# Layer 1 of a spatial CNN: adding the residual in place, permuting into the residual's own tile, and one ring of five tiles

## The chip, the cores and the metric

The kernel runs on one core of one Trainium2 chip. The metric is the device time of one execution in microseconds (us). Before the change it is 4453.58 us, the median of three runs (4452.78 to 4460.18). Profiles are of one further execution each; in them times count from the first instruction.

The core has five engines with an instruction stream each: TensorE (PE, with its weight loads PEld), VectorE (DVE), ScalarE (ACT), GpSimd (POOL) and SyncE (SP). SyncE here only issues DMAs; ScalarE issues some too, in between its own work. An issued DMA is carried out by 16 DMA engines. An instruction waits on semaphores at the head of its engine's stream, and what stands behind it in that stream waits as well.

## The reference, cut to what matters

The input is x with shape (32, 48, 64, 128): batch, channels, height H, width W, in float32. Two layers follow each other, with different weights. Each is a residual block:

```python
x = x + scnn(group_norm(x, 16 groups))       # layer 0
x = x + scnn(group_norm(x, 16 groups))       # layer 1

def step(w, b):
    def f(carry, inp):
        nxt = inp + conv1d(carry, w, b)      # 5 taps, 48 -> 48 channels, padding 2
        return nxt, nxt
    return f
# scnn: down over H, up over H (same weights), right over W, left over W
```

Each of the four passes is a scan: row h needs the finished row h-1 (or h+1), and column v needs v-1 (or v+1). The convolution of a row step runs along the width, that of a column step along the height. So the work is a chain of 126 row steps and 254 column steps for each group of batches, and a step is a small matrix product followed by an addition.

## The kernel before, in words

Batches are taken in groups of eight (GB), four groups. Row phases treat one group, column phases treat two groups (a pair) at once. The list PHASES gives twelve phases: eight of rows and four of columns; the last two are ("cols", 1, 0) and ("cols", 1, 1), the column scans of layer 1 for the first and for the second pair. With these alone the change is concerned. A scan step is nine matmuls (L647), which add into three PSUM tiles, and three VectorE instructions (L656), which add bias and the old value and write the new column over it in SBUF.

SBUF holds one large tile, the arena: three slots, and behind them a stage of four tiles of 128 x 2048 float32 (1 MB each). A column phase needs its whole width at once in the scan to the right and again in the scan to the left, but there are four quarters of the width (j = 0 to 3) and only three slots. So quarter 0 is written out to DRAM (spill_unit) after its part of the right scan, quarter 3 takes its slot, and in the left scan, when quarter 3 is finished and its results are out, quarter 0 is read back into that slot. The next column phase loads its quarters 0, 1 and 2 (load_unit) into the slots of the finished phase as these come free.

The left scan finishes quarter 3 first, then 2, 1, 0. A quarter consists of six units (UNITS: three channel groups times the two batch groups of the pair) of 128 x 2048 values. For each unit of layer 1 the finished values, in the order of the scan, have to be added to the residual (the layer's input, kept in DRAM as "mid") and brought into the order of the output, in which the eight columns of a block lie side by side. Before, one function does both, add_permuted (L606 to 610): eight GpSimd additions of 128 x 256 each read the scan's values and the residual with permuted strides, and write into a tile perm. The residual lies in one of three tiles nat: two of the stage and a spare one in the memory of the row weights (downs), which layer 1 no longer needs then. The two other stage tiles are perm.

What then happens to perm depends on the phase. In the last phase, and for quarter 3 of the phase before it, store_result (L618) writes it straight to the output in DRAM, in runs of 32 float32 (128 bytes). For quarters 2, 1 and 0 of the first of the two phases, hold_result (L626) writes it as one block of 1 MB to a DRAM buffer (held), issued by ScalarE, and let_result (L630) copies it from there to the output during the next phase. store_result and let_result are issued by SyncE, and so are load_unit and spill_unit. load_residual (L578) is issued by ScalarE in layer 1, three or four DMAs a unit.

The last quarter of the last phase (j = 0, when TensorE has ended) has a treatment of its own. last_loads (L880) loads its six residuals into the slot of the finished quarter 2. last_results (L884) adds them on VectorE in place, then copies each unit in eight slices into a stage tile, by ScalarE, GpSimd and VectorE in turn (L894), and stores it.

The order of each engine's instructions is written out by hand, by an agenda. `at(t, fn, ...)` puts a piece of work at time t, counted in scan steps, not in microseconds; before each step the main loop traces all pieces that are due, and in_order (L196) makes each engine keep this order. The times thus fix the order within each engine's stream only; when a piece really runs is decided by semaphores. In plan_cols (L796) `left` is the step at which the left scan begins. The units of layer 1 stand at left + 34 + 32 per quarter + 4.5 per unit; the first residuals at left + 16; the following ones 4.9 after the unit that frees their tile; a store or hold 5 after its unit; the spill reads of quarter 0 at left + 64 and 2 steps apart; last_loads at left + 97, just ahead of the units of quarter 1.

Every DMA of the built program also waits for an earlier one: eight completion semaphores are used in turn, so a DMA waits for the eighth before it in program order, whichever queue that one is on.

Of the kernel before, what the change touches and what calls it, by code (L numbers as in the profile page):

```python
# [31 lines left out]
ALU = mybir.AluOpType  # L32
# [59 lines left out]
def kernel(  # L92
# [8 lines left out]
    nc = tc.nc  # L101
    B, _, H, W = x.shape
    NK = W // E8
    NH = H // E8
# [5 lines left out]
    UNIT = NH * LINE  # L110
# [22 lines left out]
    def const(shape, name):  # L133
        return cpool.tile(shape, F32, tag=name, name=name)
# [3 lines left out]
    stage = arena[:, 3 * SLOT :].rearrange("p (i n) -> p i n", i=4)  # L138
    wt = {k: const([FULL, NG, NG * FULL], f"w{k}") for k in ("right", "left")}
    downs = const([FULL, 2, NG, NG * FULL], "downs")  # L140
    wt |= {f"down{i}": downs[:, i] for i in range(2)}
    bd = const([FULL, NG, 2, 3], "bd")
    mask_sb = const([P, P], "mask_sb")
    maskp = const([P, NG, FULL], "maskp")
# [74 lines left out]
    def slots(k):  # L219

        return (0, 1, 2) if k % 2 == 0 else (2, 1, 0)
# [327 lines left out]
    UNITS = [(g, half) for g in range(NG) for half in range(2)]  # L549

    def quarter(k, j):
        return slot[slots(k)[j % 3]].rearrange("p (o s n) -> p s o n", s=2, o=NG)
# [29 lines left out]
        for e, c0, c1, p0 in pieces(o):  # L582
            dma(nat[p0 : p0 + c1 - c0], by_col(t, e, j)[c0:c1], nc.scalar if layer else None)

    def add_residual(k, j, i, nat):
        o, half = UNITS[i]
        unit = quarter(k, j)[:, half, o]
        nc.gpsimd.tensor_tensor(unit, unit, nat, ALU.add)  # L588

    def keep_result(k, j, i):  # L590
        _, layer, pair = PHASES[k]
# [7 lines left out]
    def by_image(t):  # L599

        return t.rearrange("p (a e k b) -> p a b k e", a=NH, e=E8, b=GB)

    def by_w(t):
        return t.rearrange("p (a b k e) -> p a b k e", a=NH, b=GB, e=E8)

    def add_permuted(k, j, i, nat, perm):  # L606
        o, half = UNITS[i]
        res = by_image(quarter(k, j)[:, half, o])
        for a in range(NH):
            nc.gpsimd.tensor_tensor(by_w(perm)[:, a], res[:, a], by_image(nat)[:, a], ALU.add)  # L610

    def in_output(j, g, e):

# [4 lines left out]
    def store_result(k, j, i, perm):  # L618
        pair = PHASES[k][2]
        o, half = UNITS[i]  # L620
        for e, c0, c1, p0 in pieces(o):
            dst = in_output(j, 2 * pair + half, e)[c0 * NH : c1 * NH]
            src = perm[p0 : p0 + c1 - c0].rearrange("p (a b n) -> p a b n", a=NH, b=GB)
            dma(dst.rearrange("(c a) b n -> c a b n", a=NH), src)
# [166 lines left out]
    def follows(k):  # L791

        _, layer, pair = PHASES[k]
        return PHASES[k - 1] == ("rows", layer, 2 * pair + 1)

    def plan_cols(k, t0, prev):  # L796
        _, layer, pair = PHASES[k]
        n = 2 * NG
        after = prev == "cols"
        for i in range(n):  # L800
            if follows(k) and UNITS[i][1] == 1:
                other = nc.scalar
# [12 lines left out]
            at(t0 + 50 + 2 * i, load_unit, k, 3, i)  # L815
        final = k == len(PHASES) - 1
        left = t0 + W - 1
        end = left + W - 1
        for i in range(n):
            at(left + 64 + 2 * i, spill_unit, k, i, True)  # L820
        units = []
        for n_done, j in enumerate((3, 2, 1, 0)):
            every = 4.5
            if j == 0 and PHASES[k + 1 if not final else k][0] == "rows":
                every = 7
            units += [(left + 34 + 32 * n_done + every * i, j, i) for i in range(n)]
        stats = None
        if layer == 0:
            stats = ResultStatsV(f"r{2 * pair}"), ResultStatsA(f"r{2 * pair + 1}")
        tiles = [stage[:, i] for i in range(4)]  # L830
        nats, perms = (tiles, None) if layer == 0 else (tiles[0:2], tiles[2:4])
        if layer:
            nats.append(downs.rearrange("p i g n -> p (i g n)")[:, 0:UNIT])
        ahead = len(nats)

        for u, (t, j, i) in enumerate(units):
            nat = nats[u % ahead]
            o, half = UNITS[i]
            if u < ahead:
                at(left + 16, load_residual, k, j, i, nat)  # L840
            elif not (final and j == 0):
                at(units[u - ahead][0] + (3 if layer == 0 else 4.9), load_residual, k, j, i, nat)
            if layer == 0:
                at(t, add_residual, k, j, i, nat)
                at(t + 4, keep_result, k, j, i)
                unit = quarter(k, j)[:, half, o]
                if half == 0:
                    for b in range(GB):
                        at(t + 5 + b, stats[0].take, j, o, unit, b)
                else:  # L850
                    at(t + 1, stats[1].take, j, o, unit)
            elif not (final and j == 0):
                perm = perms[u % 2]
                at(t, add_permuted, k, j, i, nat, perm)
                if final or j not in HELD:
                    at(t + 5, store_result, k, j, i, perm)
                else:
                    at(t + 5, hold_result, j, i, perm)
        if layer == 0:
            t = units[-1][0] + 14  # L860
            g = 2 * pair
            spread(t, scaling(f"r{g}", 1, g, stats[0], r_masks), 1)
            spread(t + 20, scaling(f"r{g + 1}", 1, g + 1, stats[1], r_masks), 1)
        if layer:

            at(left + 10, nc.scalar.copy, junk[:, 0:1], quarter(k, 3)[:, 0, 0, RUN - 1 : RUN])
        if layer and not final:
            todo = [(j, half, e) for j in HELD for half in range(2) for e in range(E8)]
            for n, what in enumerate(todo):
                at(end + 63 + 1.9 * n, let_result, *what)  # L870
        if final:
            at(left + 97, last_loads, k)
            at(end + 4, last_results, k)

    def last_tiles(k):

        s = slot[slots(k)[2]].rearrange("p (i n) -> p i n", i=2 * NG)
        return [s[:, i] for i in range(2 * NG)]
# [5 lines left out]
    def last_results(k):  # L884

        for i, nat in enumerate(last_tiles(k)):
            o, half = UNITS[i]
            unit = quarter(k, 0)[:, half, o]
            nc.vector.tensor_tensor(unit, unit, nat, ALU.add)
            perm = stage[:, i % 4]  # L890
            for a in range(NH):
                eng = (nc.scalar, nc.gpsimd, nc.vector)[a % 3]
                copy = eng.copy if eng is nc.scalar else eng.tensor_copy
                copy(by_w(perm)[:, a], by_image(unit)[:, a])  # L894
            store_result(k, 0, i, perm)


# [3 lines left out]
    for k, (kind, layer, _) in enumerate(PHASES):  # L901
        (plan_rows if kind == "rows" else plan_cols)(k, starts[k], PHASES[k - 1][0])

    def wide_nat(i0, n):
        return arena[0:P, i0 : i0 + GB * n * W].rearrange("p (b m) -> p b m", b=GB)

    tiles = [stage[0:P, i] for i in range(4)]
    nats1 = [wide_nat(2 * SLOT + i * UNIT * 4, 8) for i in range(2)]
    plan_input(1, [starts[0] + 38 + 13 * j for j in range(4)], 11, 5, nats1, tiles[2:4])
    nats = [wide_nat(3 * SLOT, 4)]  # L910
# [214 lines left out]
```

## Time and profile before

| what | before |
|---|---|
| median of three runs | 4453.58 us |
| the profiled execution | 4463.67 us, span 4461.9 us |
| TensorE busy | 4157.1 us, 93% of the span |
| GpSimd additions of add_permuted (L610) | 336 of about 1.09 us |
| ScalarE copies of last_results (L894) | 18 of 0.65 us |
| last matmul ends | 4337.8 us |
| DMA moved | 680 MB, mean 152 GB/s |

How to read what follows. The page gives for every engine the busy time, its share and the number of instructions. It cuts the span into 40 equal slices of 111.5 us and prints the busy share of each in tenths. A group line gives source line, engine, operation, output and inputs with shapes and the number of instructions; after the bar the busy time and the mean of one in ns; after the next bar the idle time of the engine just before them and what ended most of it. A timeline line gives start, length, and in brackets the idle time before with what released it. The waits list says who waited for whom, with total, number and longest. In the table of windows each row is a stretch of the span: its length, busy time and (count) of the engines, granted TensorE clock, busy share of the 16 DMA engines and GB/s. The names tell the phase: step_10r and step_10l are the right and left scans of layer 1's first pair, step_11r and step_11l those of the second.

### The profile page before, as it was taken

The page shows a single profiled execution, that of the slowest core. Times are in us where ns is not written, and L with a number is a line of the kernel's source. Part 1 is how long each engine was busy: PE and PEld are TensorE (multiplying, and loading weights), DVE is VectorE, ACT ScalarE, POOL GpSimd, SP SyncE. Part 2 cuts the span into 40 slices and gives each one's busy share as a digit, 9 for nine tenths or more (in the row PEclk, how much of TensorE's full clock was granted, in tenths as well). Part 3 has the DMA queues.
Part 4 walks back from the last instruction along what each step waited for, and adds up shares of the span by engine and source line. Part 5 has one row for each costly group of instructions (what it writes and reads, how often), then busy time and mean ns, then how long its engine had stood idle before and what let it go on. Part 6 is the DMA issues. An engine that isn't in the chain of part 4 may idle for free.

```text
span 4461.9 us, 89843 instructions
## 1 busy us (share of the span) xinstructions
PE 4157.1 (93%) x36632; PEld 4127.5 (93%) x36632; DVE 2187.4 (49%) x6594; ACT 1190.5 (27%) x2360; POOL 908.3 (20%) x943
## 2 busy tenths in 40 slices
PE   4899997999999999998999999999999999999980
PEld 1799997999999999998999999999999999999980
DVE  5354443446655444444446654444444444444442
ACT  1743301434785545100006765403000000000000
POOL 3342000324322020000004410000000035520544
PEclk9999998999999999999999999999999999999995
DMA  8989789856988989578308989658295059999799
GB/s 175 177 166 154 124 145 180 226 112 194 228 185 143 156 158 158 94 126 201 67 1 252 212 167 145 104 82 147 44 161 138 1 108 256 245 225 160 140 183 159
DMA packets 2111229, 680.33 MB, mean 152 GB/s; under 512 B 2000992, under 2 KB 2053984, under 8 KB 2070880
## 3 DMA queue, kind: packets, MB, share of 16 engines
q1 hardware_dynamic: 2095168, 599.07, 70.5%
q10 hardware_dynamic: 15648, 75.51, 6.8%
q8 instruction: 288, 4.72, 0.5%
q14 instruction: 125, 1.02, 0.1%
HBM read 397.57 MB, written 295.98 MB: 155 GB/s over the span
## 4 chain that ended last, share of the span: by engine, by line
PE 79%; DMA 10%; SPq 3%; POOL 3%; ACT 3%; issue 1%; DVE 1%; ACTq 0%; POOLq 0%; DVEq 0%
PE step_01r L647 6%; PE step_00r L647 6%; PE step_10r L647 6%; PE step_00l L647 6%; PE step_01l L647 6%; PE step_11l L647 4%; PE step_10l L647 3%; SPq L192 3%; PE step_11r L647 3%; PE step_11d L647 3%; PE step_11u L647 3%; PE step_10u L647 3%; PE step_12d L647 3%; PE step_13u L647 3%; PE step_13d L647 3%; PE step_03d L647 3%
## 5 line engine op out<-in xcount | busy, mean ns | idle before, releaser
L535 ACT ACTIVATE arena<-arena,offset,scale 128x256 f32<-128x256 f32 (+2 forms) x864 | 601.0, 789 | 435.7 <-DMA arena<-mid 210.0
L492 POOL COPY arena<-arena 112x256 f32<-112x256 f32 x458 | 270.5, 645 | 756.8 <-DMA arena<-in_x 512.6
L610 POOL TENSOR_TENSOR arena<-arena 128x256 f32<-128x256 f32 x224 | 234.8, 1092 | 782.9 <-DVE arena L656 672.1
L588 POOL TENSOR_TENSOR arena<-arena 128x2048 f32<-128x2048 f32 x48 | 217.7, 4561 | 841.4 <-PE step_01l L647 537.1
L426 ACT ACTIVATE junk<-arena 128x256 f32<-128x256 f32 x192 | 129.5, 675 | 694.7 <-POOL arena L588 688.6
L647 PE MATMUL step_00r<-arena,wright 128*128 128x128 f32 x2286 | 257.5, 276 | 27.6 <-DMA arena<-upa 27.6
L647 PEld LDWEIGHTS step_00r<-arena,wright 128*128 128x128 f32 x2286 | 257.1, 193 | 27.9 <-issue 27.7
L647 PE MATMUL step_01r<-arena,wright 128*128 128x128 f32 x2286 | 258.7, 277 | 24.4 <-DMA arena<-upa 24.4
L647 PEld LDWEIGHTS step_01r<-arena,wright 128*128 128x128 f32 x2286 | 258.4, 194 | 24.8 <-issue 24.6
L201 ACT COPY junk<-arena 128x1 f32<-128x1 f32 x2 | 0.4, 192 | 1043.7 <-DMA out<-held 526.5
L647 PE MATMUL step_11r<-arena,wright 128*128 128x128 f32 x2286 | 260.2, 278 | 11.1 <-DVE arena L656 11.1
L647 PEld LDWEIGHTS step_11r<-arena,wright 128*128 128x128 f32 x2286 | 259.7, 194 | 11.5 <-DVE arena L656 11.5
L647 PE MATMUL step_00l<-arena,wleft 128*128 128x128 f32 x2286 | 256.3, 275 | 0.0
L647 PE MATMUL step_10r<-arena,wright 128*128 128x128 f32 x2286 | 256.1, 275 | 0.0
L647 PEld LDWEIGHTS step_10r<-arena,wright 128*128 128x128 f32 x2286 | 255.7, 192 | 0.3
L647 PEld LDWEIGHTS step_00l<-arena,wleft 128*128 128x128 f32 x2286 | 255.7, 192 | 0.0
L647 PE MATMUL step_10l<-arena,wleft 128*128 128x128 f32 x2286 | 255.4, 275 | 0.0
L647 PE MATMUL step_01l<-arena,wleft 128*128 128x128 f32 x2286 | 255.4, 275 | 0.0
L647 PE MATMUL step_11l<-arena,wleft 128*128 128x128 f32 x2286 | 255.4, 275 | 0.0
L647 PEld LDWEIGHTS step_10l<-arena,wleft 128*128 128x128 f32 x2286 | 255.4, 192 | 0.0
L647 PEld LDWEIGHTS step_01l<-arena,wleft 128*128 128x128 f32 x2286 | 255.3, 192 | 0.0
L647 PEld LDWEIGHTS step_11l<-arena,wleft 128*128 128x128 f32 x2286 | 255.3, 192 | 0.0
(175 smaller groups left out, 7124.1 us busy)
## 6 DMA issues: line engine op xcount, KB each, us to landing
xin<-arena SPq DMA_DIRECT2D x96, 384.0 KB, 5.4
arena<-xin SPq DMA_DIRECT2D x96, 384.0 KB, 8.6
mid<-arena SPq DMA_DIRECT2D x96, 384.0 KB, 7.9
arena<-mid SPq DMA_DIRECT2D x192, 192.0 KB, 4.3
upb<-arena SPq DMA_DIRECT2D x192, 192.0 KB, 3.9
arena<-upb SPq DMA_DIRECT2D x96, 384.0 KB, 11.7
arena<-xin SPq DMA_DIRECT2D x186, 192.0 KB, 4.3
upa<-arena SPq DMA_DIRECT2D x180, 192.0 KB, 3.9
```

Source lines behind the costliest of these rows:

```text
L192: (queue or nc.sync).dma_start(dst, src)
L201: fn(*args)
L426: nc.scalar.activation(junk[:, 0:n], view[:, b], AF.Identity, accum_out=self.sum[:, i, j : j + 1])
L492: copy(dst[:, r, q], src[:, r0 + r, q])
L535: nc.scalar.activation(args[0], args[0], AF.Identity, bias=args[2], scale=args[1])
L588: nc.gpsimd.tensor_tensor(unit, unit, nat, ALU.add)
L610: nc.gpsimd.tensor_tensor(by_w(perm)[:, a], res[:, a], by_image(nat)[:, a], ALU.add)
L647: nc.tensor.matmul(part(whole(ps[o]), -s), weights[:, i, FULL * (o - NG * s - i + 1) : FULL * (o - NG * s - i + 2)], part(src(i), s), star ...
```

## The change

add_permuted goes. A unit of layer 1 is now added in place by add_residual: one GpSimd addition of 128 x 2048, plain strides, into the arena. Then permute_unit, a new function taken out of last_results, copies the sum in eight slices of 128 x 256 into the tile that had held the residual: slices 0, 3 and 6 by GpSimd, the five others by ScalarE. From there it is stored or held as before.

There are no separate output tiles any more: five tiles, the four of the stage and the spare one, each take a residual, then the permuted result, and are free again when its store has landed. The first five residuals are loaded at left + 16. Residual u + 3 goes into the tile of unit u - 2, and its load stands after the store of unit u. On ScalarE the order becomes: copies of unit u, its hold (where there is one), load of residual u + 3, copies of unit u + 1. The copies of units 12 to 17 of the last phase come after last_loads there. last_results keeps its three engines and takes its output tiles from the same five. Layer 0 is planned as before.

```diff
+    spare_tile = downs.rearrange("p i g n -> p (i g n)")[:, 0:UNIT]
...
-    def add_permuted(k, j, i, nat, perm):
+    def permute_unit(k, j, i, perm, engines):
+
         o, half = UNITS[i]
-        res = by_image(quarter(k, j)[:, half, o])
+        src = by_image(quarter(k, j)[:, half, o])
         for a in range(NH):
-            nc.gpsimd.tensor_tensor(by_w(perm)[:, a], res[:, a], by_image(nat)[:, a], ALU.add)
+            eng = engines[a % len(engines)]
+            copy = eng.copy if eng is nc.scalar else eng.tensor_copy
+            copy(by_w(perm)[:, a], src[:, a])
...
-        nats, perms = (tiles, None) if layer == 0 else (tiles[0:2], tiles[2:4])
         if layer:
-            nats.append(downs.rearrange("p i g n -> p (i g n)")[:, 0:UNIT])
-        ahead = len(nats)
-
-        for u, (t, j, i) in enumerate(units):
-            nat = nats[u % ahead]
+            tiles.append(spare_tile)
+        n = len(tiles)
+        direct = [u for u in units if not (final and u[1] == 0)]
+
+        for u, (t, j, i) in enumerate(direct):
+            nat = tiles[u % n]
             o, half = UNITS[i]
-            if u < ahead:
+            if u < n:
                 at(left + 16, load_residual, k, j, i, nat)
...
-            elif not (final and j == 0):
-                perm = perms[u % 2]
-                at(t, add_permuted, k, j, i, nat, perm)
+            else:
+
+                at(t, add_residual, k, j, i, nat)
+                at(t + 2.5, permute_unit, k, j, i, nat, (nc.gpsimd, nc.scalar, nc.scalar))
                 if final or j not in HELD:
-                    at(t + 5, store_result, k, j, i, perm)
+                    at(t + 4.5, store_result, k, j, i, nat)
                 else:
-                    at(t + 5, hold_result, j, i, perm)
+                    at(t + 4.5, hold_result, j, i, nat)
+
+                if u >= 2 and u - 2 + n < len(direct):
+                    at(t + 4.6, load_residual, k, *direct[u - 2 + n][1:], tiles[(u - 2) % n])
...
         for i, nat in enumerate(last_tiles(k)):
-            o, half = UNITS[i]
-            unit = quarter(k, 0)[:, half, o]
-            nc.vector.tensor_tensor(unit, unit, nat, ALU.add)
-            perm = stage[:, i % 4]
-            for a in range(NH):
-                eng = (nc.scalar, nc.gpsimd, nc.vector)[a % 3]
-                copy = eng.copy if eng is nc.scalar else eng.tensor_copy
-                copy(by_w(perm)[:, a], by_image(unit)[:, a])
+            perm = (*(stage[:, n] for n in range(4)), spare_tile)[i % 5]
+            add_residual(k, 0, i, nat, nc.vector)
+            permute_unit(k, 0, i, perm, (nc.scalar, nc.gpsimd, nc.vector))
             store_result(k, 0, i, perm)
```

More of the change, by code (lines that the diff above doesn't have):

```diff
@@ L583, in load_residual, with add_residual @@
             dma(nat[p0 : p0 + c1 - c0], by_col(t, e, j)[c0:c1], nc.scalar if layer else None)
-    def add_residual(k, j, i, nat):
+    def add_residual(k, j, i, nat, eng=nc.gpsimd):
         o, half = UNITS[i]
         unit = quarter(k, j)[:, half, o]
-        nc.gpsimd.tensor_tensor(unit, unit, nat, ALU.add)
+        eng.tensor_tensor(unit, unit, nat, ALU.add)
     def keep_result(k, j, i):
@@ L830, in plan_cols @@
         tiles = [stage[:, i] for i in range(4)]
-        nats, perms = (tiles, None) if layer == 0 else (tiles[0:2], tiles[2:4])
         if layer:
-            nats.append(downs.rearrange("p i g n -> p (i g n)")[:, 0:UNIT])
-        ahead = len(nats)
-        for u, (t, j, i) in enumerate(units):
-            nat = nats[u % ahead]
+            tiles.append(spare_tile)
[3 more added lines that the diff above has]
+            nat = tiles[u % n]
             o, half = UNITS[i]
-            if u < ahead:
+            if u < n:
                 at(left + 16, load_residual, k, j, i, nat)
-            elif not (final and j == 0):
-                at(units[u - ahead][0] + (3 if layer == 0 else 4.9), load_residual, k, j, i, nat)
             if layer == 0:
+                if u >= n:
+                    at(direct[u - n][0] + 3, load_residual, k, j, i, nat)
                 at(t, add_residual, k, j, i, nat)
@@ L851, in plan_cols @@
                     at(t + 1, stats[1].take, j, o, unit)
-            elif not (final and j == 0):
-                perm = perms[u % 2]
-                at(t, add_permuted, k, j, i, nat, perm)
+            else:
+                at(t, add_residual, k, j, i, nat)
+                at(t + 2.5, permute_unit, k, j, i, nat, (nc.gpsimd, nc.scalar, nc.scalar))
                 if final or j not in HELD:
-                    at(t + 5, store_result, k, j, i, perm)
+                    at(t + 4.5, store_result, k, j, i, nat)
                 else:
-                    at(t + 5, hold_result, j, i, perm)
+                    at(t + 4.5, hold_result, j, i, nat)
+                if u >= 2 and u - 2 + n < len(direct):
+                    at(t + 4.6, load_residual, k, *direct[u - 2 + n][1:], tiles[(u - 2) % n])
         if layer == 0:
```

## The prediction

> **What bounds the kernel now.** I read the page first: TensorE is busy 93% of the span, and both its own row and the DMA row of the 40 slices are near full in the second half of layer 1.
>
> ```profile
> PE 4157.1 (93%) x36632; PEld 4127.5 (93%) x36632; DVE 2187.4 (49%) x6594; ACT 1190.5 (27%) x2360; POOL 908.3 (20%) x943
> PE   4899997999999999998999999999999999999980
> DMA  8989789856988989578308989658295059999799
> ```
>
> TensorE is therefore not what the change can shorten; only places where it waits, and the stretch after it has ended, are. The timeline of TensorE over the two column phases of layer 1 names them (start, length, group, idle before it):
>
> ```profile
> 3811.22 65.38 PE L647 MATMUL step_11r<-arena,wright 128*128 128x128 f32 x584
> 3880.09 66.25 PE L647 MATMUL step_11r<-arena,wright 128*128 128x112 f32 x576 [3.50 <-DVE arena L656]
> 3953.92 128.58 PE L647 MATMUL step_11r<-arena,wright 128*128 128x112 f32 x1126 [7.58 <-DVE arena L656]
> 4082.34 255.43 PE L647 MATMUL step_11l<-arena,wleft 128*128 128x128 f32 x2286
> ```
>
> The last phase halts twice, 3.50 + 7.58 = 11.1 us, and TensorE ends at 4082.34 + 255.43 = 4337.8, which leaves 124.1 us of tail. GpSimd's timeline tells what those halts wait for: units of the phase before (u0 to u23, six per quarter of the width).
>
> ```profile
> 3692.57 8.34 POOL L610 TENSOR_TENSOR arena<-arena 128x256 f32<-128x256 f32 x8 [5.44 <-DVE arena L656]
> 3855.61 8.31 POOL L610 TENSOR_TENSOR arena<-arena,downs 128x256 f32<-128x256 f32 x8 [5.80 <-issue]
> 3934.59 8.31 POOL L610 TENSOR_TENSOR arena<-arena,downs 128x256 f32<-128x256 f32 x8
> 4399.24 8.63 POOL L610 TENSOR_TENSOR arena<-arena,downs 128x256 f32<-128x256 f32 x8 [1.72 <-DMA out<-arena]
> ```
>
> u6 starts at 3692.57, u17 ends at 3863.9 and u23 at 3942.9. Each quarter of the arena may be refilled for the next phase only when its six units are through; the refill lands at 3880 and 3953.9, and TensorE goes on. In the tail the 18th unit ends at 4407.9. The waits of GpSimd from 4140 to the end, and the busy table (TensorE, weight load, VectorE, ScalarE, GpSimd, clock, DMA share, GB/s), say what holds the units:
>
> ```profile
> POOL arena L610 <- DMA out<-arena: 57.6, 6, 18.3
> POOL arena L610 <- DMA arena<-mid: 18.7, 2, 13.7
> 3700.00:3750.00 50.00, 50.00 (x450) 50.00 (x449) 23.99 (x75) 0.00 (x0) 25.82 (x25) 1.00 1.01 291
> 4240.00:4260.00 20.00, 20.00 (x182) 20.00 (x180) 9.61 (x30) 0.00 (x0) 0.00 (x0) 1.00 0.98 200
> 4300.00:4320.00 20.00, 20.00 (x182) 20.00 (x181) 9.54 (x30) 0.00 (x0) 11.21 (x11) 1.00 0.79 143
> 4400.00:4420.00 20.00, 0.00 (x0) 0.00 (x0) 8.37 (x6) 3.49 (x6) 17.41 (x20) 0.50 0.77 122
> ```
>
> GpSimd waits for stores that still read its two output tiles, and the 16 DMA engines are full (0.97 to 1.04) from 3700 to 4100 and nearly so in the tail, where gaps of a fifth appear from 4280 to 4320 and after 4380. So the tail is a queue of DMA work with some holes, and the drain before it is a queue of DMA work that began late.
>
> **What the Trainium skill says.** "DMA: Bandwidth & Descriptors", section "Issuing engines are not separate DMA queues": transfers started by ScalarE and SyncE run on the same 16 engines and interleave. The trace agrees: from 3860 to 3950 the two queues hold 52.6% and 45.8% of the same engines. "GPSIMD Engine Reference", section "3.1 Elementwise": an fp32 add of 2048 elements takes 4497 ns on GpSimd; the trace has 4561 ns (L588). "SBUF — State Buffer", section "Who interferes with whom": VectorE contends with GpSimd's reads only if it has two SBUF inputs or runs in a two-port mode. The scan's VectorE row reads one operand from PSUM, and 348 ns each in L656 beside GpSimd's adds fits that; so a longer GpSimd add should not slow the scan.
>
> **The change, part by part.** Three rows price the engines:
>
> ```profile
> L588 POOL TENSOR_TENSOR arena<-arena 128x2048 f32<-128x2048 f32 x48 | 217.7, 4561 | 841.4 <-PE step_01l L647 537.1
> L610 POOL TENSOR_TENSOR arena<-arena 128x256 f32<-128x256 f32 x224 | 234.8, 1092 | 782.9 <-DVE arena L656 672.1
> L894 ACT COPY arena<-arena 128x256 f32<-128x256 f32 x18 | 10.8, 646 | 324.9 <-DMA arena<-mid 287.5 <-DMA out<-arena 28.2 <-POOL arena L610 9.1
> ```
>
> (1) Engines. A unit costs GpSimd 8 x 1.04 = 8.3 us now. After: one plain add, 4.56, then three copies at 0.70 (median of L894 on GpSimd) = 6.7 us; beside those, five copies on ScalarE, 5 x 0.65 = 3.2 us. A unit is complete 4.56 + 3.2 = 7.8 us after its start, against 8.3. That alone is worth nothing while the engines wait for DMA; the 42 adds and copies stay hidden under it. VectorE's part at the very end changes only its tile order.
>
> (2) Tiles. Now three tiles take residuals and two take outputs; a unit needs the store two before it landed. After, five tiles do both. Residual u+3 is loaded when store u-2 has landed, and stands on ScalarE between the copies of unit u and of u+1. So ScalarE's copies of u+1 wait, in effect, for that store and for the loads' issue. Two bounds for that loop: the built program lets every DMA wait for the eighth before it, which brings the wait nearer to store u-1; so two units per (copies 3.2 + store landing + issue). Landing of a held store is 14.2 us (median), issuing three or four loads took 2 to 8.6 us: 19.6 to 26 us, 9.8 to 13 us a unit. Before, u6 to u23 took 3942.9 - 3692.6 = 250 us, 13.9 a unit. The loop is therefore not the limit, DMA is; I keep both ends for the range.
>
> (3) Preload. Five residuals instead of three are fetched while DMA is idle (share 0.26 from 4120 to 4140; in the first phase likewise before 3618). From 4140 to the end the loading queue moved 22.0 MB, 21 units, at 29.5% of 322 us = 95 us, so 4.5 us each: 2 x 4.5 = 9 us leave the tail.
>
> (4) First drain. Units u0 to u4 no longer wait for loads: from 3618.0, five units at 6.7 us reach 3651; u5's residual goes out when store 0 lands (3626 + 10.9 = 3637), arrives some 7 us later, and u5 is done by about 3660, not 3687. So u6 starts when its columns are ready, 3618.0 + 64 (32 steps of 2.01) = 3682, and not at 3692.6: 10 us. The six spill reads of 1 MB that SyncE issues next went out from 3698; they now go from about 3662, out of the full stretch. That stretch moved some 66 MB in 250 us, 0.27 MB/us; 6 MB of spill and 2 MB of residuals less are 30 us. At the loop's worst 13 us a unit, u23 ends at 3682 + 7 + 18 x 13 = 3923, and TensorE needs it 6 us before 3942.8 (where it would be without the first halt); at the DMA's pace it is some 20 us earlier still. Both halts should go. I take 10 of 11.1 us.
>
> (5) Tail. All DMA work from 4140 is 0.905 x 322 = 291 us, and the first store starts at 4152.7, 309 us before the end: 18 us are holes. A hole is refilled if a further store or load is ready; the five-deep ring does that for most units. What stays: the 20 loads of the last quarter stand on ScalarE ahead of the copies of u12, so stores pause until they are issued, and the final stores have a start and a landing. I take half, 9 us, as gained. With the preload: 18 us. The six spill reads that TensorE needs at 4275.8 went out from 4224 to 4262; SyncE issues them behind store 5, which comes earlier, so they are no new wait; on SyncE stores and spill reads keep their order. The last six units go round five tiles instead of four, so only the sixth waits for a store of its own round: one landing of some 7 us, under four stores that are still in the queue, is counted at nothing.
>
> Sum: 10 + 18 = 28 us. The profiled execution took 4463.7 us (span 4461.9 and 1.8 around it), 10 us over the median of 4453.6; I assume its waits are those of the timed runs. 4453.6 - 28 = 4425.6.
>
> **Rivals.** *Half of it* (0.14): DMA at 1.0 from 3700 is a bound that no ring removes; if the halts stay, only the tail's 18 us come, 4435.6; if the holes stay and only the halts go, 4443.6. *All of it* (0.11): the holes close wholly and the last stores follow each other without pause: 11 + 9 + 18 = 38, 4415, and a few us less if packets of loads and stores overlap as well as in 4320 to 4380 (shares of 1.11 to 1.19): down to 4406. *No change* (0.09): the copies on ScalarE open as many holes as the tiles close; 4445 to 4460. For it speaks that the last loads took ScalarE from 4319 to 4378. *Slower* (0.08): copies queue behind DMA issue on ScalarE. If a unit takes 16 us in place of 13.9, u23 ends at 3682 + 288 = 3970 and TensorE halts 34 us, 23 more than now; the tail's twelve later units lose 12 x 1.5 = 18 and gain 9: together +32, 4485. It decides from 14.5 us a unit, 29 us for two; my worst pair is 26. Against it: store landing would have to grow, with the same bytes in flight.
>
> **How the numbers follow.** The forecast has 0.58 and by itself spans 4412 to 4437. A difference of 0.2%, 8.9 us, is about the least that can be told from none here. Faster: 0.58 + 0.14 + 0.11 = 0.83; within: 0.09; slower: 0.08. The range 4406 to 4450 holds the forecast, the halves, the full gain and part of no change.
>
> **What would show it.** After: GpSimd's adds read 128x2048 at 4.5 to 4.7 us in layer 1, ScalarE has 210 more copies near 0.65 us; u5 of the first column phase ends near 3660; no halt over 1 us in step_11r; TensorE ends near 4328; from there to the end about 106 us, with DMA shares above 0.9 until the last 20 us. Wrong would be: ScalarE's copies waiting for loads while DMA shares fall below 0.8 after 4300, a halt in step_11l for the spill, or the same halts in step_11r at full DMA.

## The result, and the profile after

The changed kernel takes 4435.51 us (median of five runs, 4428.66 to 4442.85) against 4457.17 us before (five runs, 4452.78 to 4462.11). The ratio is 0.9952 with a 95% interval of 0.9935 to 0.9968: 0.5% less time, 21 us, between 14 and 29. A later measurement of the same kernel, beside other runs, gave 0.9937 (0.9922 to 0.9951). The forecast was 4425.6 us, 28 us less than before, in a range of 4406 to 4450.

The page of the kernel after, first its busy times, DMA row and costliest group on GpSimd:

```profile
PE 4160.7 (94%) x36632; PEld 4130.6 (93%) x36632; DVE 2184.7 (49%) x6594; ACT 1311.7 (30%) x2570; POOL 828.6 (19%) x775
DMA  8988879865997989678406989839187059999899
L589 POOL TENSOR_TENSOR arena<-arena 128x2048 f32<-128x2048 f32 x83 | 376.4, 4549 | 1743.6 <-PE step_01l L651 508.5
```

ScalarE has 210 instructions more (2570 against 2360), GpSimd 168 fewer and 80 us less work. The addition takes 4549 ns. The timeline of TensorE over the last phase:

```profile
3817.76 130.30 PE L651 MATMUL step_11r<-arena,wright 128*128 128x128 f32 x1160
3952.33 128.77 PE L651 MATMUL step_11r<-arena,wright 128*128 128x112 f32 x1126 [4.27 <-DVE arena L660]
4080.93 255.47 PE L651 MATMUL step_11l<-arena,wleft 128*128 128x128 f32 x2286
```

The first halt is gone, the second is 4.27 us in place of 7.58. TensorE ends at 4336.4; the span is 4441.1, so the tail, from there to the end, is 104.7 us instead of 124.1. In this execution the column phases of layer 1 began at 3306.6, 6.6 us later than in the profile before, in code that the change does not touch. I therefore compare stretches that start at the first matmul of step_10r: 1161.9 us before, 1134.5 after, 27.4 less. Of these 7.9 lie before the last matmul and 19.4 in the tail. A second profile of the kernel after has 1130.9, with a halt of 4.56 and a tail of 100.5, so single profiles differ by some 4 us. Of the kernel before there is one profile only, and its execution (4463.67 us) was longer than all five timed ones; the differences to it in what follows can therefore be some us too large, as 27.4 against 21 by the medians.

The shorter halts account for 6.8 of the 7.9 us. The rest lies just behind the halts, where TensorE comes back slowly. This is the kernel before, behind its second halt:

```profile
3953.90:3960.00 6.10, 6.08 (x32) 6.08 (x33) 1.98 (x6) 0.00 (x0) 0.00 (x0) 0.58 1.00 193
```

In these 6.1 us TensorE does 32 matmuls at a granted clock of 0.58; in the next 10 us it does 92 at 1.00.

GpSimd's timeline of the kernel after, with the additions of u5, u6 and u23 of the first pair and of the 18th unit in the tail:

```profile
3658.76 4.57 POOL L589 TENSOR_TENSOR arena<-arena 128x2048 f32<-128x2048 f32 x1
3691.16 4.53 POOL L589 TENSOR_TENSOR arena<-arena 128x2048 f32<-128x2048 f32 x1 [25.95 <-PE step_10l L651]
3930.77 4.53 POOL L589 TENSOR_TENSOR arena<-arena 128x2048 f32<-128x2048 f32 x1 [7.98 <-DMA arena<-mid]
4360.50 4.49 POOL L589 TENSOR_TENSOR arena<-arena 128x2048 f32<-128x2048 f32 x1 [4.46 <-ACT arena L614]
```

u6 now waits 25.95 us for its columns: the first quarter is through long before. But from u6 to u23 it takes 3930.77 - 3691.16 = 239.6 us, 14.1 a unit, the same pace as before (3934.59 - 3692.57 = 242.0, 14.2 a unit). In the tail the table of windows and the waits show where time is still lost:

```profile
4140.00:4160.00 20.00, 20.00 (x182) 20.00 (x181) 9.61 (x30) 5.78 (x10) 14.55 (x9) 1.00 0.28 46
4202.93:4212.93 10.00, 10.00 (x92) 10.00 (x92) 4.75 (x16) 0.00 (x0) 3.29 (x1) 1.00 0.46 73
4322.93:4332.93 10.00, 10.00 (x92) 10.00 (x91) 4.81 (x15) 2.87 (x5) 0.00 (x0) 1.00 0.67 147
4360.00:4380.00 20.00, 0.00 (x0) 0.00 (x0) 0.00 (x0) 3.27 (x6) 6.26 (x4) 0.50 0.76 121
```

```profile
POOL arena L589 <- DMA arena<-mid: 56.8, 3, 39.7
ACT arena L614 <- DMA out<-arena: 59.6, 6, 16.8
POOL arena L589 <- DMA out<-arena: 15.9, 2, 10.0
SPq L193 <- DMA downs<-mid: 14.9, 2, 13.1
```

DMA (the share before the last number) still has holes, a new one among them from 4203 on. The second profile has it too, at the same distance from the start of the left scan (0.46); the hole after 4323 it has not (1.02). GpSimd's additions hardly wait for stores any more (15.9 us against 57.6), but for residuals. Of ScalarE's 59.6 us, 36 pass ahead of copies because the loads in front of them in its stream fill tiles again, and wait for stores; the rest are waits of the last quarter's copies for their output tiles. The last line, from 4190 to 4232, shows where the new hole comes from. SyncE waits up to 13.1 us, until 4217.3, with a store of u5 for a load of ScalarE; ScalarE issued that load at 4214.29, behind the first copy of u6, which had waited for the scan. So the two queues hold each other up.

### The profile page after: what moved, and what is told of

The parts are those of the page before. It is cut to its first block, busy times and chain, and to the rows that moved or that the text cites. A ratio compares the mean times of both kernels' runs of the same rounds, so it can differ in the third digit from the quotient of the medians.

```text
span 4441.1 us, 89969 instructions
## 1 busy us (share of the span) xinstructions
PE 4160.7 (94%) x36632; PEld 4130.6 (93%) x36632; DVE 2184.7 (49%) x6594; ACT 1311.7 (30%) x2570; POOL 828.6 (19%) x775
## 3 DMA queue, kind: packets, MB, share of 16 engines
q14 instruction: 125, 1.02, 0.1%
## 4 chain that ended last, share of the span: by engine, by line
PE 84%; DMA 6%; SPq 4%; ACT 2%; DVE 1%; issue 1%; POOL 1%; ACTq 0%; POOLq 0%; DVEq 0%
PE step_00r L651 6%; PE step_01r L651 6%; PE step_10r L651 6%; PE step_00l L651 6%; PE step_10l L651 6%; PE step_01l L651 6%; SPq L193 4%; PE step_11r L651 4%; PE step_11l L651 4%; PE step_10u L651 3%; PE step_11u L651 3%; PE step_13d L651 3%; PE step_12u L651 3%; PE step_12d L651 3%; PE step_03d L651 3%; PE step_10d L651 3%
## 5 line engine op out<-in xcount | busy, mean ns | idle before, releaser
L589 POOL TENSOR_TENSOR arena<-arena 128x2048 f32<-128x2048 f32 x83 | 376.4, 4549 | 1743.6 <-PE step_01l L651 508.5
L651 PE MATMUL step_01r<-arena,wright 128*128 128x128 f32 x2286 | 258.0, 276 | 23.5 <-DMA arena<-upa 23.5
L651 PEld LDWEIGHTS step_01r<-arena,wright 128*128 128x128 f32 x2286 | 257.7, 193 | 23.9 <-issue 23.7
L614 ACT COPY arena<-arena 128x256 f32<-128x256 f32 x190 | 109.7, 655 | 477.2 <-POOL arena L589 215.4
L358 ACT ACTIVATE junk<-arena 112x512 f32<-112x512 f32 x160 | 100.9, 631 | 491.0 <-DMA arena<-in_x 486.6
```

The lines of the kernel that those rows point to most:

```text
L358: nc.scalar.activation(junk[0:P], piece, AF.Identity, accum_out=self.sum[:, at[0], at[1]],)
L589: eng.tensor_tensor(unit, unit, nat, ALU.add)
L614: copy(by_w(perm)[:, a], src[:, a])
L651: nc.tensor.matmul(part(whole(ps[o]), -s), weights[:, i, FULL * (o - NG * s - i + 1) : FULL * (o - NG * s - i + 2)], part(src(i), s), star ...
```

## The experiments

Theory at first, as in the prediction: the engines are hidden, the gain comes from earlier DMA work (preload, first drain) and from holes that a deeper ring closes. The main rival is that ScalarE, which now holds copies and DMA issues in one stream, costs more than allowed for. All kernels were timed against the kernel before on the same chip; the medians of before were 4459.34, 4448.79 and 4454.53 us in the three groups of runs, so ratios are to be compared, not times. "Stretch" is the time from the first matmul of step_10r to the end, from one profile.

| run | time, us | ratio to before (95%) | stretch, us | halts in step_11r, us | tail, us |
|---|---|---|---|---|---|
| before | 4457.17 | 1 | 1161.9 | 3.5 + 7.6 | 124.1 |
| after | 4435.51 | 0.9952 (0.9935 to 0.9968) | 1134.5 | 4.3 | 104.7 |
| after, again | 4427.77 | 0.9937 (0.9922 to 0.9951) | 1130.9 | 4.6 | 100.5 |
| new work, old tiles | 4448.00 | 0.9975 (0.9968 to 0.9981) | 1150.4 | 7.1 | 118.8 |
| three tiles | 4476.13 | 1.0036 (1.0022 to 1.0050) | 1172.2 | 22.3 | 124.9 |
| three preloaded | 4433.32 | 0.9942 (0.9927 to 0.9957) | 1128.9 | 6.3 | 97.7 |
| copies on GpSimd | 4416.76 | 0.9905 (0.9890 to 0.9919) | 1110.6 | none | 87.1 |
| copies on GpSimd, old tiles | 4431.03 | 0.9959 (0.9944 to 0.9974) | 1129.6 | none | 107.4 |
| loads before copies | 4425.18 | 0.9946 (0.9930 to 0.9963) | 1130.4 | 5.5 | 100.3 |
| last loads spread | 4423.45 | 0.9941 (0.9926 to 0.9956) | 1126.5 | 5.7 | 96.0 |
| both orders | 4425.01 | 0.9934 (0.9919 to 0.9950) | 1128.5 | 6.0 | 97.6 |
| copies on GpSimd, ScalarE waits | 4417.21 | 0.9912 (0.9896 to 0.9927) | 1117.4 | none | 93.4 |
| copies on GpSimd, last loads spread | 4410.31 | 0.9897 (0.9881 to 0.9914) | 1116.3 | none | 92.7 |
| copies on GpSimd, no last loads | 4387.26 | 0.9862 (0.9848 to 0.9877) | 1086.2 | none | 63.2 |

The four kernels with five tiles and all copies on GpSimd have a short new halt elsewhere, of 0.5 to 1.4 us in step_10l.

### The new work with the old tiles

```diff
-            tiles.append(spare_tile)
+            tiles = [*tiles[0:2], spare_tile]
         n = len(tiles)
+        perms = [stage[:, 2], stage[:, 3]]
...
-                at(t + 2.5, permute_unit, k, j, i, nat, (nc.gpsimd, nc.scalar, nc.scalar))
+                perm = perms[u % 2]
+                at(t + 2.5, permute_unit, k, j, i, perm, (nc.gpsimd, nc.scalar, nc.scalar))
...
+                if u + n < len(direct):
+                    at(t + 4.9, load_residual, k, *direct[u + n][1:], tiles[u % n])
...
```

> The new division of the work (one GpSimd addition in place, three copies on GpSimd, five on ScalarE) with the old tiles: three for residuals, two for results, three preloaded. Theory (the gain is DMA work that starts earlier and holes that a deeper ring closes; the engines are hidden): the tail after the last matmul stays near 124 us (118 to 128, before 124.1), the halts of step_11r near 11 us (6 to 12, before 11.1), the time within 8 us of before. Rival (the shorter unit, 7.8 us instead of 8.3, and the freed GpSimd make the gain): tail near 105 us and halts near 4, as in the kernel after (104.7 and 4.3).

Halt and tail lie in the theory's ranges, at their lower ends, but the time falls by 0.25%, 11 us (8 to 14), and the stretch by 11.5. So the division of the work is worth something by itself. u6 starts 384.6 us after the first matmul of step_10r, as in the kernel after (before: 392.5), and the first halt is gone here too. The group rows of this run, from 3600 to the end, say how:

```profile
L589 POOL TENSOR_TENSOR arena<-arena 128x2048 f32<-128x2048 f32 x28 | 127.1, 4539 | 653.5 <-PE step_10l L651 446.4 <-PE step_11l L651 207.1
L614 POOL COPY arena<-arena 128x256 f32<-128x256 f32 x144 | 94.6, 696 | 309.3 <-DMA out<-arena 170.1 <-DMA held<-arena 124.0 <-DMA arena<-spill 8.6
```

The additions wait for the scan alone; the wait for a result tile, which in the kernel before stood in front of the permuting addition, stands in front of the copies. Read with the code, adding in place lets a unit take in its residual, and give the residual's tile back for the next load, before a result tile is free. The arena itself serves as one more buffer. That it is not the shorter unit is shown below by the run with old tiles in which a unit is longer than before.

### Three tiles in the ring

```diff
-            tiles.append(spare_tile)
+            tiles = tiles[0:3]
...
-                    at(t + 4.6, load_residual, k, *direct[u - 2 + n][1:], tiles[(u - 2) % n])
+                    at(t + 4.4, load_residual, k, *direct[u - 2 + n][1:], tiles[(u - 2) % n])
```

> The kernel after with three tiles in its ring in place of five; the residual of unit u + 1 is loaded when the store of unit u - 2 has landed, so nothing is preloaded beyond the third. Theory (DMA is the bound, the ring matters only through the preload and the holes): three units per landing 8 to 14, load 7 and unit 7.8 us, that is 8 to 10 us a unit in the tail against 11 us of DMA work a unit; the tail is 9 us of preload and some holes longer than after, 114 to 122 us; halts 4 to 12 us. Rival (the depth of the ring sets the pace): tail above 124 us, halts above 11 us, the time above that of before.

The rival is right. The kernel is slower than before by 0.36% (0.22 to 0.50), and the first pair's drain carries it (waits of that stretch):

```profile
POOL arena L589 <- DMA arena<-mid: 82.7, 10, 12.0
PE step_11r L651 <- DVE arena L660: 22.3, 1, 22.3
```

Each unit waits for its residual, the residual for a store. The units u3, u4 and u5 start at 3652.0, 3665.4 and 3679.0, 13.5 us apart, although their columns were ready; I had put 8 to 10 on that loop. The depth of the ring does set the pace, and a loop worked out from the landings of single DMAs came out too short.

### Three residuals preloaded

```diff
-            if u < n:
+            if u < (n if layer == 0 else 3):
                 at(left + 16, load_residual, k, j, i, nat)
+            elif u < n:
+                at(direct[u - 3][0] + 4.6, load_residual, k, j, i, nat)
```

> The kernel after, but only three residuals are loaded ahead of each left scan's results; the fourth and fifth follow the stores of the first and second unit. Theory: 2 x 4.5 = 9 us of DMA work come back into the tail: 110 to 116 us after the last matmul (after 104.7), halts 4 to 7 us, the time 6 to 12 us above the kernel after. Rival (the preload is hidden anyway, since the first units wait for the scan): tail 103 to 107, the time as after.

Nothing is lost: ratio 0.9942, tail 97.7. The preload of two more residuals was worth nothing here. Two windows of the run with three preloaded show why; its left scan begins within 0.2 us of that of the kernel after, so they can be held against the same times above:

```profile
4140.00:4160.00 20.00, 20.00 (x181) 20.00 (x180) 9.61 (x30) 5.83 (x10) 14.43 (x9) 1.00 0.53 87
4200.00:4220.00 20.00, 20.00 (x182) 20.00 (x181) 9.51 (x31) 2.90 (x5) 10.18 (x5) 1.00 0.97 172
```

The first share rises from 0.28 to 0.53, and the second from 0.62 in the kernel after to 0.97. The loads run, or push other transfers to run, where the DMA engines were short of work in any case.

### All copies on GpSimd

```diff
-                at(t + 2.5, permute_unit, k, j, i, nat, (nc.gpsimd, nc.scalar, nc.scalar))
+                at(t + 2.5, permute_unit, k, j, i, nat, (nc.gpsimd,))
```

> The kernel after with all eight copies of a unit on GpSimd, so a unit costs 4.55 + 8 x 0.61 = 9.4 us there and ScalarE issues its loads without standing copies. Theory (DMA is the bound): tail 101 to 110 us (after 104.7), halts 2 to 7 us (after 4.3), the time within 6 us of after. Rival 1 (copies queued behind the loads' issue on ScalarE cost much, the 37 us of the last twenty loads above all): tail 85 to 95 us. Rival 2 (the engines' time for a unit counts): tail 115 us or more.

The first rival's number is right: a tail of 87.1. There is no halt in step_11r, and the time is 0.95% below before, though a unit now occupies GpSimd for 9.3 us instead of 6.4. Its left scan begins 12.8 us earlier than in the kernel after, so these windows match the two holes shown above. The second view is the addition of u23 in GpSimd's timeline:

```profile
4190.14:4200.14 10.00, 10.00 (x92) 10.00 (x92) 4.75 (x16) 0.00 (x0) 3.35 (x1) 1.00 0.97 180
4310.14:4320.14 10.00, 10.00 (x92) 10.00 (x91) 4.80 (x15) 0.00 (x0) 0.00 (x0) 1.00 1.16 217
```

```profile
3897.24 4.52 POOL L589 TENSOR_TENSOR arena<-arena 128x2048 f32<-128x2048 f32 x1
```

Both holes are closed. u6 starts at 3684.67 in this run, so u6 to u23 takes 212.6 us, 12.5 a unit instead of 14.1. In the kernel after, the timelines of ScalarE and SyncE in the same stretch show a wait that stood in the way (start, length, what; ACTq and SPq are their issuing of DMAs):

```profile
3870.37 17.46 ACTq L193 DMA_DIRECT2D arena<-mid  x4
3887.87 2.89 ACT L614 COPY downs<-arena 128x256 f32<-128x256 f32 x5 [19.55 <-issue]
3895.49 0.34 ACTq L193 DMA_DIRECT2D held<-downs  x1
3879.77 1.76 SPq L193 DMA_DIRECT2D spill<-arena  x3
```

The four loads of one residual take 17.46 us to issue, since each waits for an earlier DMA; the copies of the next unit, whose sum was ready at 3865.3, stand behind them until 3887.87, and its hold until 3895.49. The DMA engines were not full in that time: none of them worked from 3874 to 3880. The second load waited 13 us for the first of SyncE's writes to spill. That write had itself waited for the scan, was issued at 3879.77 and landed at 3883.66; the load follows at 3883.68.

Which DMA waits for which changed together with the copies, and no run holds it fixed. A DMA waits for the one before it on its completion semaphore. By the semaphores that the traces keep, 36 of the 81 DMAs that ScalarE issues from 3600 to 3960 wait for one of SyncE's in the kernel after, also in its repetition and in the three runs on the order below. With five tiles and all copies on GpSimd it is 11 or 12. With the old tiles it is 41 of 88 with split copies, 12 with GpSimd's, and 12 in the kernel before. So the run shows what taking the copies off ScalarE brings, but not whether it is the copies' place behind the issues or these fewer waits for SyncE that brings it.

### Copies on GpSimd with the old tiles

The two edits above together: three tiles for residuals, two for results, all copies on GpSimd.

> All eight copies on GpSimd, as in the run that gave 87 us, but with the old tiles: three for residuals, two for results, three preloaded. Theory (a result tile is free only when its store has landed, so two of them leave holes whatever engine copies): tail 105 to 119 us, halts 3 to 11 us. Rival (ScalarE's stream is the whole matter, the ring none): tail 85 to 92 us and no halt.

The halts are gone as with five tiles, the tail is 107.4 us. So for the halts the step from split copies to GpSimd's is the whole matter, and for a good part of the tail the ring is: both the theory and the rival are half right. A unit takes 4.53 + 8 x 0.59 = 9.3 us on GpSimd here, longer than the 8.3 us before, and yet the kernel takes 0.41% (0.26 to 0.56) less time than before: it is the separation of addition and copy that counts, not the length of a unit. ScalarE copies as little in these units here as before, and waits for SyncE's DMAs as often, so these two cannot be the reason. The four kernels form a square, in us gained on before by their ratios (of 4455 us): old tiles 11 with split copies and 18 with GpSimd's; five tiles 21 to 28 with split copies and 42 with GpSimd's. By the stretches they are 11.5, 32.3, 27.4 to 31.0 and 51.3. The sizes are uncertain by some 10 us. By either measure five tiles gain on the old ones whatever engine copies, and GpSimd's copies gain on split ones whatever the tiles; whether old tiles with GpSimd's copies or five tiles with split ones are better, the two measures do not agree.

### The order in ScalarE's stream: three runs

Loads before copies:

```diff
-                if u >= 2 and u - 2 + n < len(direct):
-                    at(t + 4.6, load_residual, k, *direct[u - 2 + n][1:], tiles[(u - 2) % n])
+                if u >= 3 and u - 3 + n < len(direct):
+                    at(t + 2.4, load_residual, k, *direct[u - 3 + n][1:], tiles[(u - 3) % n])
```

> The kernel after with one thing changed in ScalarE's stream: the load of a later residual (u + 2, into the tile of unit u - 3) stands ahead of the copies of unit u, not behind them. Theory (revised after the copies on GpSimd alone gave 87 us of tail: loads stand behind copies that wait for the scan, and hold up the DMA queues; in the kernel after ScalarE stood 25.7 us before the copies of the seventh unit and the DMA engines were idle from 4208 to 4214): most of the difference between 104.7 and 87.1 us comes back, tail 88 to 97 us, the halt of step_11r under 3 us. Rival (the copies wait behind the loads' issue, in the last twenty loads above all): tail 101 to 108 us.

Last loads spread:

```diff
-            at(left + 97, last_loads, k)
+            for i, nat in enumerate(last_tiles(k)):
+                at(left + 98 + 4.5 * i + 4.7, load_residual, k, 0, i, nat)
```

> The kernel after, with the twenty loads of the last quarter's residuals no longer in one block ahead of the copies of the thirteenth unit, but three or four behind each of the units 12 to 17. Theory (loads behind waiting copies are what costs): little or a loss, tail 102 to 110 us, since the loads now stand behind more copies. Rival (the block of 37 us in front of the copies costs): tail 88 to 97 us. The halt stays within 3 us of 4.3 in both.

Both at once:

> The kernel after with its split copies and both repairs of ScalarE's order at once: each load ahead of the copies of its unit, and the last twenty loads spread behind units 12 to 17. If the two losses are separate they add: 4 and 8 us gave 1130.4 and 1126.5 us against 1134.5, so 1120 to 1126 us from the first matmul of step_10r to the end. If any order of DMA issues and copies in one stream costs about the same, 1126 to 1134. The halt of step_11r stays (3 to 7 us) in both cases, since in the drain of the first pair copies then wait for the loads.

The first edit does less than was meant. In the kernel after, the load of unit u + 2 stands behind the copies of unit u - 1, and so ahead of those of unit u already. The edit moves it to just before the copies of unit u, and between the two places ScalarE has nothing else to do. In the traces ScalarE's stream of the first drain is the same in both kernels: five copies, a hold, three or four loads, five copies. Only at the block of twenty is the order another: the load of u14 stands behind the block instead of ahead of it. So its tail of 100.3 and its stretch of 1130.4, those of the second profile of the kernel after (100.5 and 1130.9), say nothing about the revised theory, and the run with both edits is in the main the spread block alone.

Spreading the block gave a tail of 96.0, at the rival's edge, and with both edits 97.6; that is 3 to 9 us less than the two profiles of the kernel after, which themselves differ by 4. The ratio with both (0.9934) is like that of the kernel after measured beside it (0.9937). The halt remains in all three. A stream in which the loads really stand ahead of the copies that they now follow was not run.

### ScalarE waits, but copies nothing that a store needs

```diff
+                at(t + 2.5, nc.scalar.copy, junk[:, 0:1], quarter(k, j)[:, half, o, 0:1])
```

added to the kernel with all copies on GpSimd.

> All copies on GpSimd and five tiles, as in the run with 87 us of tail; but at the place of its former five copies ScalarE copies one column of the unit, which nobody reads, so that its DMA issues again stand behind a wait for each unit's addition, while no store waits for ScalarE. Theory A (loads and holds that stand behind such a wait are the loss): most of the 24 us between split copies and GpSimd's comes back, segment from the first matmul of step_10r to the end 1125 to 1136 us. Theory B (copies that stand behind the issue of DMAs are the loss): nothing changes, 1106 to 1115 us (1110.6 without the waits, 1134.5 in the kernel after).

The waits are there, as ScalarE's timeline of this run shows; a load is issued only behind each:

```profile
4194.49 0.19 ACT L202 COPY junk<-arena 128x1 f32<-128x1 f32 x1 [17.67 <-POOL arena L589]
4194.56 2.10 ACTq L193 DMA_DIRECT2D downs<-mid  x4
```

Yet the halts stay away and the ratio is 0.9912, within its interval the same as without the waits (0.9905). The stretch of 1117.4 lies nearer to 1110.6 than to 1134.5, a little over theory B's range. In this kernel, then, issues behind a wait for each addition cost at most a few us. That speaks for the opposite cause, copies that a store or a refill needs standing behind DMA issues, as in the lines from 3870 on above. It does not prove it: here too only 12 of ScalarE's 81 DMAs wait for SyncE's, so the fewer waits between the queues remain as a rival. They would also explain why the halt stayed in all three runs on the order. A kernel with split copies and few such waits, which would decide, was not run.

### How far DMA is the floor

```diff
-            at(left + 97, last_loads, k)
```

taken from the kernel with all copies on GpSimd.

> All copies on GpSimd and five tiles, and the residuals of the last quarter are not loaded at all (the last six units add what their tiles hold). That takes 6 MB, some 6 x 4.5 = 27 us of DMA work, out of the tail. Theory (with the copies on GpSimd the tail is a full DMA queue): the tail falls from 87 us by 18 to 27 us, to 60 to 69. Rival (the tail is set by the last units' chain of add, copy and store): 80 us or more.

The tail falls by 87.1 - 63.2 = 23.9 us, near the 27 of the loads left out. So with the copies on GpSimd the tail follows its DMA work, as the prediction had assumed for the kernel after. It is not full to the end: with the loads in place the DMA shares of 10 us windows lie between 1.08 and 1.22 from 4290 to 4340, and between 0.72 and 0.90 from there on.

### The last loads spread with all copies on GpSimd, and the kernel after once more

> All copies on GpSimd, five tiles, and the last twenty loads spread behind units 12 to 17. With no copies of these units on ScalarE the block holds up only the loads behind it: GpSimd waited 36.7 us for a residual then. Expected: tail 80 to 88 us (87.1 with the block), no halt; if the tail is a full DMA queue in any order, 85 to 90.

> The kernel after once more, beside the others on one chip, to see how far its tail (104.7 us) and its halt (4.3 us) repeat: if the 97.7 us of the run with three preloaded residuals was chance, this one lies between 97 and 105; the time 20 to 25 us above that of the GpSimd copies with spread loads.

Spreading makes no difference that can be measured (0.9897 against 0.9905; tail 92.7 against 87.1, the wrong way and about as much as profiles scatter). The version with copies on GpSimd, with or without it, beats both kernels; beside the repeated kernel after it took 17 us less (4410.31 against 4427.77; 20 to 25 had been expected). The repetition puts the tail at 100.5, so the 97.7 with three preloaded cannot be told from it.

## Why the prediction was right, and where its steps were not

The direction and the size hold: 28 us were forecast, 21 measured and 28 in the repetition. The two places were right as well: halts 10 us shorter forecast, 6.8 measured; tail 18 us shorter forecast, 19.4 and 23.6 measured. But the steps behind these sums fared unevenly, and errors cancelled: that the sum came so close is in part luck.

- Step 1, the engines: "That alone is worth nothing while the engines wait for DMA." It failed. With the old tiles the new division is worth 11 us. The working compared lengths of a unit, 7.8 against 8.3 us, and overlooked that adding in place moves the wait for the result tile from the addition to the copies.
- Step 2, the loop: "19.6 to 26 us, 9.8 to 13 us a unit" and "The loop is therefore not the limit, DMA is". The range failed: the drain kept 14.1 us a unit, and with three tiles, where I expected 8 to 10, units came 13.5 apart. DMA was nearly the limit, with a share of 0.95 from u6 to u23, but waits between the queues left holes in it. With the copies off ScalarE the units' own loads and holds (32.2 MB in both kernels) went at 12.5 us a unit, while SyncE's queue moved 23.5 MB instead of 28.3.
- Step 3, the preload: "9 us leave the tail." It failed: three preloaded residuals give the same time.
- Step 4, the first drain: that u5 is done in time and u6 starts when its columns are ready held (u5's addition ends at 3663.3). Counted from the first matmul of step_10r, u6 starts at 384.6 instead of 392.5, 8.0 us earlier (10 forecast). The reason was another: the run with the old tiles and three preloaded has the same 384.6, so the separation of addition and copy gave it, not the five residuals. That the spill reads "now go from about 3662, out of the full stretch" failed:

```profile
3705.50 22.62 SPq L193 DMA_DIRECT2D arena<-spill  x6
```

That is 398.9 us after the first matmul of step_10r, against 398.3 before. SyncE stood 18.1 us ahead of them, with the last store of u5, for a load that ScalarE issued behind copies of u6. So the drain kept this work, the pace did not improve, and the second halt shrank only to 4.3 us where I had it gone.

- Step 5, the holes: I took half of 18 us, by the ring. The ring does more than that: between old and five tiles the tail falls by 14 to 18 us with split copies and by 20 with GpSimd's. This and the 5 us of tail that the separation alone gives (118.8 against 124.1) made up for the 9 us of preload that did not come.

Of the rivals, "Slower" named a wait that the traces show, copies queued behind DMA issue on ScalarE, and said it would decide from 14.5 us a unit. The drain stayed just below that, at 14.1. Taking the copies off ScalarE brought 14 to 24 us more; how much of this is that wait, and how much the fewer waits for SyncE's DMAs, stays open. "No change" gave ScalarE's 59 us of last loads as its sign; the block takes 37 us after and its spreading moved the tail by 4 to 9 us.

## What to carry to other kernels

When work is moved onto an engine that also issues DMAs, count what will stand behind those issues, and what the issues wait for: here one residual's loads held ScalarE for 17.46 us, 13 of them for a write in SyncE's queue that waited for the scan, while eight copies on the other engine cost 4.7. Splitting an operation that needs two buffers at once into one that works in place and one that moves the result frees the first buffer early, even if the parts together take longer. And a loop bound put together from single landings came out too short here (9.8 to 13 us against 14.1, and 8 to 10 against 13.5); the pace of the same stretch before the change, 14.2 us a unit, was the safer price.

## What the runs showed of the hardware that was not expected

GpSimd and ScalarE took the same time for these permuting copies: eight of 128 x 256 in 4.7 us on GpSimd, 0.59 each, and five in 2.9 us on ScalarE, 0.58 each. The permuting addition of the same size had taken GpSimd 1.04 us.
